# Routed expert weights: two loads for each of two matrices instead of one

## The chip, the cores and the metric

The kernel runs on one core of one Trainium2 chip. The metric is the device time of one execution in microseconds (us); lower is better. The profile that is shown is one execution, recorded by the hardware profiler. The engines are named as in the profile: PE is TensorE (matrix products), PEld its loads of the stationary operand, DVE VectorE, ACT ScalarE, POOL GpSimd, SP the engine that issues most DMA transfers. A "q" behind a name (SPq) means that engine's instruction queue: its issues and waits. DMA queue q1 is the one that SP's transfers go through, q0 the one of GpSimd's indirect transfers; both are carried by the same 16 DMA engines (the rings, below).

## What is computed

Two layers on 2048 tokens of 512 values, everything in 32-bit floats. The first layer is an RWKV recurrence gated by a two-expert feed-forward; the second is an attention gated by a mixture of experts. The change touches the loads of the mixture alone:

```python
h = relu(einsum('td,ndf->ntf', flat, shared_w1) + shared_b1[:, None, :])
shared_out = einsum('ntf,nfd->td', h, shared_w2) + shared_b2.sum(0)
out = flat + shared_out
scores = sigmoid(flat @ centroids.T) + bias
vals, idx = top_k(scores, KR)                      # KR = 4 of NR = 16 experts
gating = zeros_like(scores).at[arange(T)[:, None], idx].set(vals)
gating = gating / clip(gating.sum(-1, keepdims=True), 1e-08)
def step(acc, ew):
    w1, b1, w2, b2, g = ew                         # w1: 512 x 352, w2: 352 x 512
    hj = relu(flat @ w1 + b1)
    yj = hj @ w2 + b2
    return (acc + yj * g[:, None], None)
rout, _ = scan(step, zeros_like(flat), (routed_w1, routed_b1, routed_w2, routed_b2, gating.T))
return (out + rout).reshape(b, s, d)
```

The result of the layer is x + attention * silu(mixture).

## The kernel before

The kernel is written with a framework that takes tiles and their uses, puts the instructions of each engine in order by a planner with estimated costs, and adds the waits. Blocks under a runtime condition are kept as one piece.

The first layer takes the span up to about 900 us, the carrying over and the routing up to 1200, the shared experts and the keys of the attention up to 1350. Then comes the stage that matters here.

*Routed experts, 1353 to 1920 us.* Each token has four experts, so there are 2048 * 4 rows, sorted by expert into tiles of 128 rows in the DRAM tensor `xs`. There are at least 64 tiles (`FULL_TILES`) and at most 80 (`NRT`); the last ones run only if they are needed (L1722 and after). In this execution 73 results were written. For tile j, `hidden_rows(j)` (L1648):

- reads the number of the tile's expert into a register of SP;
- loads that expert's weights with `load1` (L650): `w1` as 128 partitions of 4 x 352 values (5632 B of each partition lie together in memory), `w2` as 128 partitions of 2 x 512 values (4096 B together), `w3`, the last 96 rows of the second matrix (2048 B each), and one row with the bias, in four transfers on SP's queue (L655 to L658). The pool `m1w` (L1527) holds three tiles' weights, so the load for tile j waits until tile j - 3 has been used: w1 until its product at L1676 is done, w2 and w3 until that at L1700 is done;
- loads the rows `x` (L1662, four buffers), turns them on PE (L1669), copies them (`xg`, L1671, ACT), multiplies by w1 in three parts of 128, 128 and 96 columns (L1676) with a relu on ACT behind each (`ht`, L935);
- makes on DVE each row's gate `g` (L1684) and its row number in the output (`to`, L1694, six buffers).

`down_rows(j)` (L1697), one tile later, multiplies by w2 and w3 (L1700), scales by the gate on DVE (`y`, L1705, four buffers), and adds the 128 rows to the DRAM tensor `comb` with an indirect DMA on GpSimd's queue (L1706), a read-modify-write in memory. Two tiles may add to the same row, so the framework lets these scatters follow each other one at a time.

Between the tiles stand 34 steps of the attention (`AHEAD`, L1712), which PE, ACT and DVE do in between; they have loads of their own on SP's queue (cosines and sines, L1333 and L1334, and `xo`, L1740).

`load1` is also called for the two shared experts in `behind_recurrence` (L665), at about 901 us, long before their use.

In memory, the weights are laid out by partition: `a["w1"]` is (18, 128, 4, 352), `a["w2"]` (18, 128, 3, 512).

Of the kernel before, what the change touches and what calls it, by code (L numbers as in the profile page):

```python
# [21 lines left out]
NC = D // P  # L22
# [45 lines left out]
NF1 = len(FCH)  # L68
# [9 lines left out]
def tile_kernel(ctx: ExitStack, tc: tile.TileContext, a: dict):  # L78
    nc = tc.nc
# [93 lines left out]
    for i in range(0, NT, 2):  # L173
        xin = n0.tile([P, 2, D], F32, tag="xin", bufs=NT // 2, name="xin")
        nc.sync.dma_start(
            out=xin, in_=a["x"][i * P : (i + 2) * P, :].rearrange("(n p) d -> p n d", p=P)
# [10 lines left out]
        out=wdc, in0=gate0_w[:, :, 1], in1=gate0_w[:, :, 0], op=ALU.subtract  # L187
    )
    wdp = n0ps.tile([P, NC, P], F32, tag="tp", name="wdp")
    for c in range(NC):  # L190
        dg = n0.tile([P, P], F32, tag="dg", bufs=2, name="dg")
        nc.vector.tensor_scalar(
            out=dg, in0=ident, scalar1=wdc[:, c : c + 1], scalar2=None, op0=ALU.mult
# [16 lines left out]
        out=upper, in_=upper, compare_op=ALU.is_gt, fill=0.0, base=0,  # L210
# [7 lines left out]
        out=eno, in0=col[:, 0:NST], scalar1=float(P), scalar2=None, op0=ALU.mult  # L218
# [3 lines left out]
    for i in range(0, NT, 2):  # L222
# [4 lines left out]
            out=shift, in0=mv[:, :, 0], scalar=-1.0, in1=rstd, op0=ALU.mult, op1=ALU.mult  # L227
# [3 lines left out]
        for j in range(2):  # L231
# [6 lines left out]
                out=junk, in0=xn, in1=wdiff, scale=1.0, scalar=0.0, op0=ALU.mult, op1=ALU.add,  # L238
                accum_out=dl[:, i + j : i + j + 1],
            )  # L240
    for i in range(NT):
# [10 lines left out]
        out=sel[:, :, 0], in0=dl, scalar1=0.0, scalar2=None, op0=ALU.is_le  # L252
    )
    nc.vector.tensor_scalar(
        out=sel[:, :, 1], in0=dl, scalar1=0.0, scalar2=None, op0=ALU.is_gt
# [3 lines left out]
        out=m, in0=dl, scalar=-1.0, in1=dl, op0=ALU.mult, op1=ALU.min  # L259
# [8 lines left out]
    for o, tri in ((0, upper), (N2, sums)):  # L268
        nc.tensor.matmul(
            out=tab[:, o : o + N2], lhsT=tri, rhs=sel.rearrange("p n e -> p (n e)"),  # L270
# [7 lines left out]
        out=run.rearrange("p e n -> p (e n)"), data0=newrow.rearrange("p e n -> p (e n)"),  # L278
# [8 lines left out]
        out=full, in0=own.to_broadcast([P, NT // 2]), in1=eno2[:, :, 1], op=ALU.is_gt  # L287
# [4 lines left out]
        out=paired[:, 0:1], in0=paired[:, 1:2], scalar1=2.0 * P, scalar2=None, op0=ALU.mult  # L292
    )
    nc.vector.tensor_tensor(
        out=pair_e[:, 0 : NSP - 1], in0=eno2[0:1, :, 0],
# [3 lines left out]
        out=pair_e[:, NSP - 1 : NSP], in0=own[0:1, :], in1=paired[0:1, 0:1], op=ALU.is_le  # L299
    )  # L300
    nc.vector.tensor_scalar(
        out=paired[:, 1:2], in0=paired[:, 0:1], scalar1=-1.0, scalar2=float(T),
# [4 lines left out]
        out=run[:, 1, :], in0=run[:, 1, :], scalar1=paired[:, 0:1], scalar2=None, op0=ALU.add  # L307
# [3 lines left out]
        out=row, in0=within, in1=run.rearrange("p e n -> p n e"), op=ALU.add  # L311
# [3 lines left out]
        out=alone, in0=row[:, :, 0], scalar1=paired[:, 0:1], scalar2=paired[:, 1:2],  # L315
# [10 lines left out]
        out=past, in0=bc(rowf, 2, C3), in1=bc(eno, 1, C3), op=ALU.is_ge  # L326
# [6 lines left out]
        out=place, in0=at, scalar=float(-P), in1=rowf, op0=ALU.mult, op1=ALU.add  # L333
    )
    nc.vector.tensor_tensor(
        out=past, in0=bc(at, 2, C3), in1=bc(col[:, 0:NST], 1, C3), op=ALU.is_equal
# [3 lines left out]
    for f in range(3):  # L340
        nc.vector.tensor_tensor(
            out=put[:, :, f, :], in0=past, in1=bc(facts[:, f, :], 2, C3), op=ALU.mult
# [3 lines left out]
    for i0 in range(0, NT, HN):  # L346
        hot = n0.tile([P, HN, P], F32, tag="hot", bufs=2, name="hot")
        nc.vector.tensor_tensor(
            out=hot, in0=bc(place[:, i0 : i0 + HN], 2, [P, HN, P]),
            in1=bc(col, 1, [P, HN, P]), op=ALU.is_equal,  # L350
        )
        for i in range(HN):
            nc.tensor.matmul(
                out=listed, lhsT=hot[:, i, :], rhs=put[:, i0 + i],
# [295 lines left out]
    def load1(pool, e, pick, row):  # L650

        w1 = pool.tile([P, NC, F1], F32, tag=f"w1{e}", name="w1")
        w2 = pool.tile([P, NF1 - 1, D], F32, tag=f"w2{e}", name="w2")
        w3 = pool.tile([P, D], F32, tag=f"w3{e}", name="w3")
        nc.sync.dma_start(out=w1, in_=pick(a["w1"]))  # L655
        nc.sync.dma_start(out=w2, in_=pick(a["w2"])[:, 0 : NF1 - 1, :])
        nc.sync.dma_start(out=w3[0:last, :], in_=pick(a["w2"])[0:last, NF1 - 1, :])
        nc.sync.dma_start(out=w3[last : last + 1, :], in_=row(a["b2"]))  # L658
        return w1, w2, w3
# [100 lines left out]
    for t_, fill in ((m_pool, 0.0), (n_pool, MASKED)):  # L760
        nc.gpsimd.affine_select(
            out=t_, in_=t_, compare_op=ALU.is_ge, fill=fill, base=1 - MB,
# [17 lines left out]
    for t_, fill in ((m_full, 0.0), *((t_, MASKED) for t_ in n_full)):  # L780
        own = t_[:, t_.shape[1] - P :]
        nc.gpsimd.affine_select(
            out=own, in_=own, compare_op=ALU.is_ge, fill=fill, base=0,
# [39 lines left out]
    for i in range(NT):  # L823
        yg = tr.tile([P, D], F32, tag="yg", bufs=6, name="yg")
        nc.gpsimd.indirect_dma_start(
            out=yg, out_offset=None, in_=ys0,
# [14 lines left out]
    for b in range(NRB):  # L841
# [4 lines left out]
        for s in range(n):  # L846
            nc.gpsimd.tensor_tensor(  # L847
                out=xr[:, s, :], in0=xr[:, s, :], in1=acc[:, i0 + s, 0:D], op=ALU.add
# [3 lines left out]
        for s in range(n):  # L852
            i = i0 + s
            nc.vector.tensor_scalar(
                out=acc[:, i, 0:D], in0=xr[:, s, :], scalar1=mv[:, s, 0:1],
# [3 lines left out]
        if (i + 1) % (TB // P) == 0:  # L859
            t0 = i + 1 - TB // P  # L860
            pl = m1y.tile([NR, TB], F32, tag="py", name="pl")
            for c in range(NC):
                nc.tensor.matmul(  # L863
                    out=pl, lhsT=cent[:, c, :], rhs=xT[:, c, t0 * P : (i + 1) * P],
# [10 lines left out]
    for b in range(NRB):  # L875
        rows2 = slice(b * RB, (b + 1) * RB)
        if b < PER:
            k0 = b * RB // MB
            nc.vector.tensor_reduce(
                out=xsum[:, :, k0 : k0 + RB // MB],  # L880
                in_=xT[:, :, rows2].rearrange("p c (n m) -> p c n m", m=MB),
                axis=AX.X, op=ALU.add,
            )
        else:
            nc.vector.tensor_reduce(
                out=xsum[:, :, NBLK : NBLK + 1],
                in_=xT[:, :, rows2].rearrange("p c (n m) -> p c n m", m=LW),
# [23 lines left out]
        out=upper, in_=upper, compare_op=ALU.is_gt, fill=0.0, base=0,  # L911
# [52 lines left out]
    with tc.tile_pool(name="rt", bufs=1, side="right") as rt, tc.tile_pool(  # L964
# [10 lines left out]
        for dst, tri in ((within, upper), (count, sums)):  # L975
            nc.tensor.matmul(
                out=dst.rearrange("p n e -> p (n e)"), lhsT=tri,
# [6 lines left out]
            out=run.rearrange("p e n -> p (e n)"), data0=newrow.rearrange("p e n -> p (e n)"),  # L984
# [5 lines left out]
            out=full, in0=run[:, :, NT - 1 : NT].to_broadcast([P, NR, NT]),  # L990
# [6 lines left out]
            out=end, data0=sums[:, 0:NR], data1=ntl, initial=0.0, op0=ALU.mult, op1=ALU.add  # L997
# [7 lines left out]
            out=run, in0=bc(first_tile, 2, [P, NR, NT]), scalar=float(P), in1=run,  # L1005
# [4 lines left out]
            out=row, in0=within, in1=run.rearrange("p e n -> p n e"), op=ALU.add  # L1010
# [3 lines left out]
        for k in range(KR):  # L1014
            one = rt2.tile([P, NT, NR], F32, tag="one", bufs=1, name="one")
            nc.vector.scalar_tensor_tensor(
                out=one, in0=rank, scalar=float(k + 1), in1=row, op0=ALU.is_equal, op1=ALU.mult,
# [10 lines left out]
            out=acc[:, :, D : D + NR], in0=row, in1=bc(tot, 2, [P, NT, NR]), op=ALU.mult  # L1028
# [5 lines left out]
        for i in range(NT):  # L1034
            for k in range(KR):
                ins = nc.gpsimd.indirect_dma_start(  # L1036
                    out=xs,
                    out_offset=bass.IndirectOffsetOnAxis(ap=slot[:, i, k : k + 1], axis=0),
                    in_=acc[:, i, :], in_offset=None,
# [21 lines left out]
        for m0 in (0, HM):  # L1061
# [4 lines left out]
                out=past, in0=bc(tno[:, ms], 2, sh3), in1=bc(end, 1, sh3), op=ALU.is_ge  # L1066
# [3 lines left out]
                out=te[:, ms], in0=te[:, ms], scalar1=float(NR - 1), scalar2=None, op0=ALU.min  # L1070
            )
            nc.vector.tensor_tensor(
                out=past, in0=bc(te[:, ms], 2, sh3), in1=bc(tno[:, 0:NR], 1, sh3),
# [6 lines left out]
            out=ohT, in0=te[0:NR, :], scalar1=part[0:NR, :], scalar2=None, op0=ALU.is_equal  # L1080
# [3 lines left out]
        for f in range(NF1):  # L1084
            nc.tensor.matmul(
                out=bt[:, f, :], lhsT=b1T[:, f * P : (f + 1) * P], rhs=ohT, start=True, stop=True,
# [26 lines left out]
    for w_, nm in ((wva, "Wv1"), (wks, "Wk_sem"), (wkg, "Wk_geo")):  # L1113
# [9 lines left out]
        out=ls, in0=ls, scalar1=DH ** -0.5, scalar2=None, op0=ALU.mult  # L1123
    )
    nc.vector.tensor_tensor(
        out=sm_sem, in0=ls.rearrange("p (g h) -> p g h", h=4),
# [3 lines left out]
        out=sm_geo, in0=ls.rearrange("p (g h) -> p g h", h=8),  # L1130
# [6 lines left out]
    for s_, n_ in ((slice(0, NBLK), MB), (slice(NBLK, NBLK + 1), LW)):  # L1137
        nc.vector.tensor_scalar(
            out=xk[:, :, s_], in0=xsum[:, :, s_], scalar1=1.0 / n_, scalar2=None, op0=ALU.mult,
# [8 lines left out]
    for c in range(NC):  # L1148
        ins = nc.tensor.matmul(
            out=pv, lhsT=xp[:, c].rearrange("p j k -> p (j k)"), rhs=wva[:, c, :],  # L1150
# [13 lines left out]
    for j in range(LW // P):  # L1164
        pl = kps.tile([P, HKV * DV], F32, tag="ps", name="pl")
        t0 = REMOTE + j * P
        for c in range(NC):
            nc.tensor.matmul(
                out=pl, lhsT=xT[:, c, t0 : t0 + P], rhs=wva[:, c, :],
# [22 lines left out]
    for u in range(2):  # L1192
# [9 lines left out]
        out=turn[:, :, DH : DH + HD], in0=id2[:, :, DH + HD :], scalar1=-1.0, scalar2=None,  # L1202
# [31 lines left out]
    for tb in range(NRB):  # L1234
        cols = slice(tb * RB, (tb + 1) * RB)
        pg = kps.tile([P, RB], F32, tag="ps", name="pg")
        for c in range(NC):
            nc.tensor.matmul(
                out=pg, lhsT=wkg[:, c, :], rhs=xT[:, c, cols],
# [4 lines left out]
        for j, nm in enumerate(("cos", "sin")):  # L1244
# [3 lines left out]
            if nrem:  # L1248
                nc.vector.tensor_reduce(
                    out=kg[:, j, b0 : b0 + nrem // MB],  # L1250
                    in_=tab[:, 0:nrem].rearrange("p (n m) -> p n m", m=MB), axis=AX.X, op=ALU.add,
# [9 lines left out]
        out=kgn, in0=kg[:, 1, 0:KP], scalar1=-1.0, scalar2=None, op0=ALU.mult  # L1261
# [604 lines left out]
```

## Time and profile before

| | |
|---|---|
| Median of 3 runs | 1981.4 us (1971.8 to 1984.0) |
| The profiled execution | 1987.5 us, span 1985.8 us |
| Granted TensorE clock, mean | 0.979 of full speed |
| PE, DVE, ACT, POOL busy | 94%, 39%, 27%, 19% of the span |
| DMA, whole span | 199488 packets, 381.35 MB, mean 192 GB/s |
| of these, q1 (SP) | 179800 packets, 332.78 MB, 50.8% of 16 engines' span |
| and q0 (GpSimd's indirect ones) | 18272 packets, 45.62 MB, 9.9% |
| Routed experts' stage, 1353 to 1920 us | 567 us |

How to read it: the page cuts the span into 40 slices of 49.6 us and gives a digit for each, the busy share in tenths. A packet in the DMA's counts is one contiguous run. The share of 16 engines is the time that all packets of a queue took, over 16 times the window's length; in a short window it can pass 100%, since a packet is counted where it starts or ends. The chain is followed back from the last instruction, at each step to what released it. Matmuls overlap each other, and their ends are modelled, so a PE that is shown busy is not at its peak for that.

### The profile page before, as it was taken

The page shows a single profiled execution, that of the slowest core. Times are in us where ns is not written, and L with a number is a line of the kernel's source. Part 1 is how long each engine was busy: PE and PEld are TensorE (multiplying, and loading weights), DVE is VectorE, ACT ScalarE, POOL GpSimd, SP SyncE. Part 2 cuts the span into 40 slices and gives each one's busy share as a digit, 9 for nine tenths or more (in the row PEclk, how much of TensorE's full clock was granted, in tenths as well). Part 3 has the DMA queues.
Part 4 walks back from the last instruction along what each step waited for, and adds up shares of the span by engine and source line. Part 5 has one row for each costly group of instructions (what it writes and reads, how often), then busy time and mean ns, then how long its engine had stood idle before and what let it go on. Part 6 is the DMA issues. An engine that isn't in the chain of part 4 may idle for free.

```text
span 1985.8 us, 23193 instructions
## 1 busy us (share of the span) xinstructions
PE 1869.7 (94%) x8107; PEld 1294.9 (65%) x8107; DVE 779.6 (39%) x1580; ACT 531.4 (27%) x1001; POOL 371.4 (19%) x293
## 2 busy tenths in 40 slices
PE   5899999999999999999889999999999999999857
PEld 4677777777877787777334644446776666676634
DVE  8444545362627263440256444502322222222117
ACT  5113132322324232321423122221222222222214
POOL 1211121120302120200621560001111121221120
PEclk9799999999999999999899999999999999999989
DMA  7647786536562535346532551028999999998944
GB/s 249 230 148 243 240 268 219 190 106 191 168 214 89 167 95 163 113 138 228 191 111 89 213 187 58 32 75 269 278 306 273 292 286 264 259 276 234 278 90 160
DMA packets 199488, 381.35 MB, mean 192 GB/s; under 512 B 15804, under 2 KB 106428, under 8 KB 198472
## 3 DMA queue, kind: packets, MB, share of 16 engines
q1 hardware_dynamic: 179800, 332.78, 50.8%
q0 software_dynamic: 18272, 45.62, 9.9%
q10 hardware_dynamic: 1296, 1.41, 0.2%
q8 instruction: 67, 1.10, 0.2%
q14 instruction: 53, 0.43, 0.1%
HBM read 294.04 MB, written 85.72 MB: 191 GB/s over the span
## 4 chain that ended last, share of the span: by engine, by line
PE 66%; DMA 21%; DVE 5%; issue 4%; POOL 2%; ACT 2%; SPq 0%; POOLq 0%; DVEq 0%; ACTq 0%
PE pg L567 23%; DMA comb<-y,to 17%; PE py L589 11%; PE proj L414 7%; PE py L1098 4%; PE ph L1676 4%; PE ph L949 3%; PE py L1700 3%; PE pw L1583 1%; PE pl L863 1%; PE pq L1342 1%; PE pw L1467 1%; PE pq L1398 1%; POOL xr L847 1%; PE po L1458 1%
## 5 line engine op out<-in xcount | busy, mean ns | idle before, releaser
L567 PE MATMUL pg<-xg,w 128*128 128x256 f32 (+1 forms) x2304 | 494.9, 367 | 0.0
L567 PEld LDWEIGHTS pg<-xg,w 128*128 128x128 f32 x2304 | 419.0, 190 | 90.1 <-issue 41.6
L1676 PEld LDWEIGHTS ph<-xg,w 128*128 128x128 f32 (+1 forms) x1776 | 224.3, 185 | 128.6 <-ACT ht L935 64.2
L1676 PE MATMUL ph<-xg,w 128*128 128x128 f32 (+1 forms) x1776 | 245.5, 282 | 29.3 <-ACT xg L1671 14.4
L589 PE MATMUL py<-wd,hT 128*128 128x512 f32 x544 | 256.9, 593 | 3.0 <-DVE hT L574 3.0
L1700 PE MATMUL py<-w,ht 128*128 128x512 f32 (+1 forms) x438 | 219.7, 602 | 0.0
L1706 POOL DMA_INDIRECT comb<-y,to x73 | 113.8, 1559 | 459.9 <-DVE to L1694 279.9
L574 DVE TENSOR_TENSOR hT<-sg,pg 128x256 f32<-128x256 f32 (+1 forms) x144 | 57.0, 401 | 329.9 <-ACT sg L572 329.8
L572 ACT ACTIVATE sg<-pg 128x256 f32<-128x256 f32 (+1 forms) x144 | 53.4, 371 | 412.2 <-PE pg L567 411.9
L935 ACT ACTIVATE ht<-ph,b1t 128x128 f32<-128x128 f32 (+1 forms) x222 | 81.1, 365 | 296.0 <-PE ph L1676 286.7
L589 PEld LDWEIGHTS py<-wd,hT 128*128 128x128 f32 x544 | 102.1, 190 | 72.2 <-issue 61.9
L1705 DVE TENSOR_SCALAR y<-py,g 128x512 f32<-128x512 f32 x73 | 54.5, 747 | 157.2 <-PE py L1700 104.6
L1694 DVE TENSOR_TENSOR to<-junk,away 128x1 int32<-128x1 f32 x74 | 11.8, 159 | 221.7 <-DMA comb<-y,to 220.9
L1098 PE MATMUL py<-w,hT 128*128 128x512 f32 (+1 forms) x192 | 89.3, 596 | 0.0
L1700 PEld LDWEIGHTS py<-w,ht 128*128 128x128 f32 (+1 forms) x438 | 72.2, 194 | 25.8 <-issue 24.4
L949 PE MATMUL ph<-xT,w 128*128 128x512 f32 (+1 forms) x192 | 88.0, 597 | 0.1
L1036 POOL DMA_INDIRECT xs<-acc,slot x64 | 63.4, 991 | 69.2 <-DMA xs<-acc,slot 45.5
L1671 ACT COPY xg<-tp 128x512 f32<-128x512 f32 x74 | 43.2, 584 | 101.6 <-PE tp L1669 99.2
L705 PE MATMUL po<-wo,yb 128*128 128x512 f32 x128 | 61.6, 637 | 8.4 <-DVE acc L838 4.4
L414 PE MATMUL proj<-xm,wk 128*128 128x256 f32 x256 | 59.4, 386 | 3.6 <-DVE xm L404 3.6
L1342 PE MATMUL pq<-xT,wqg 128*128 128x256 f32 x224 | 56.9, 390 | 5.5 <-PEq L1724 5.5
L414 PE MATMUL proj<-xm,wv 128*128 128x256 f32 x256 | 61.5, 394 | 0.0
(416 smaller groups left out, 2180.7 us busy)
## 6 DMA issues: line engine op xcount, KB each, us to landing
w<-in_w_dram SPq DMA_DIRECT2D x76, 704.0 KB
w<-in_w_dram SPq DMA_DIRECT2D x76, 512.0 KB
w<-in_w_gate_dram SPq DMA_DIRECT2D x72, 512.0 KB
w<-in_w_up_dram SPq DMA_DIRECT2D x72, 512.0 KB
wd<-in_w_down_dram SPq DMA_DIRECT2D x72, 512.0 KB
xs<-zero SPq DMA_DIRECT2D x16, 1360.0 KB
x<-xs SPq DMA_DIRECT2D x74, 272.0 KB
w<-in_w_dram SPq DMA_DIRECT2D x76, 192.0 KB
```

What stands on the lines that cost most here:

```text
L414: nc.tensor.matmul(out=ps[:, j, :], lhsT=w_[:, c, (o0 + j) * P : (o0 + j + 1) * P], rhs=xm[:, c, :], start=(c == 0), stop=(c == NC - 1),)
L567: nc.tensor.matmul(out=pg[:, i, 0:n], lhsT=w[:, c, i * FH + f * P : i * FH + (f + 1) * P], rhs=xg[:, c, 0:n], start=(c == 0), stop=(c == N ...
L589: nc.tensor.matmul(out=p, lhsT=hT[:, u * P : (u + 1) * P], rhs=wd[:, f, :], start=first_, stop=last_,)
L705: nc.tensor.matmul(out=po, lhsT=yb[:, c, s * P : (s + 1) * P], rhs=wo[:, c, :], start=(c == 0), stop=(c == NC - 1),)
L935: nc.scalar.activation(dst, src, AF.Relu, bias=b)
L949: nc.tensor.matmul(out=ph[0:n, :], lhsT=up(w, f, n, c), rhs=xT[:, c, cols], start=(c == 0), stop=(c == NC - 1),)
L1036: ins = nc.gpsimd.indirect_dma_start(out=xs, out_offset=bass.IndirectOffsetOnAxis(ap=slot[:, i, k : k + 1], axis=0), in_=acc[:, i, :], in_ ...
L1098: nc.tensor.matmul(out=py, lhsT=hT[0:n, e, f, s * P : (s + 1) * P], rhs=down(w, f, n), start=(e == 0 and f == 0), stop=(e == NS - 1 and f ...
L1342: nc.tensor.matmul(out=pq[:, j, :], lhsT=w[:, c, w0 : w0 + P], rhs=xT[:, c, tc0], start=(c == 0), stop=(c == NC - 1),)
L1676: nc.tensor.matmul(out=ph[0:n, f, :], lhsT=up(w, f, n, c), rhs=xg[:, c, :], start=(c == 0), stop=(c == NC - 1),)
L1700: nc.tensor.matmul(out=py, lhsT=hT[0:n, f, :], rhs=down(w, f, n), start=(f == 0), stop=(f == NF1 - 1),)
L1706: nc.gpsimd.indirect_dma_start(out=comb, out_offset=bass.IndirectOffsetOnAxis(ap=to, axis=0), in_=y, in_offset=None, compute_op=ALU.add,)
```

## The change

Inside `load1`, the one transfer for w1 becomes two, over the first two and the last two of its four blocks of 352 values, and the one for w2 becomes two, one for each block of 512 values. The longest run that lies together in memory and on the partition goes from 5632 to 2816 B for w1 and from 4096 to 2048 B for w2. Tiles, buffers, bytes and the products are the same; w3 and the bias row are loaded as before. The two shared experts' loads change in the same way.

```diff
         w1 = pool.tile([P, NC, F1], F32, tag=f"w1{e}", name="w1")
         w2 = pool.tile([P, NF1 - 1, D], F32, tag=f"w2{e}", name="w2")
         w3 = pool.tile([P, D], F32, tag=f"w3{e}", name="w3")
-        nc.sync.dma_start(out=w1, in_=pick(a["w1"]))
-        nc.sync.dma_start(out=w2, in_=pick(a["w2"])[:, 0 : NF1 - 1, :])
+        for c in range(0, NC, 2):
+            nc.sync.dma_start(out=w1[:, c : c + 2, :], in_=pick(a["w1"])[:, c : c + 2, :])
+        for f in range(NF1 - 1):
+            nc.sync.dma_start(out=w2[:, f, :], in_=pick(a["w2"])[:, f, :])
         nc.sync.dma_start(out=w3[0:last, :], in_=pick(a["w2"])[0:last, NF1 - 1, :])
         nc.sync.dma_start(out=w3[last : last + 1, :], in_=row(a["b2"]))
         return w1, w2, w3
```

## The prediction

> **What bounds the kernel now.** I read the slices of the span first, then the chain that ended last, the groups, the chain in order of time, and at last the DMA queues in short windows.
>
> ```profile
> PE   5899999999999999999889999999999999999857
> DMA  7647786536562535346532551028999999998944
> PE 66%; DMA 21%; DVE 5%; issue 4%; POOL 2%; ACT 2%; SPq 0%; POOLq 0%; DVEq 0%; ACTq 0%
> L1706 POOL DMA_INDIRECT comb<-y,to x73 | 113.8, 1559 | 459.9 <-DVE to L1694 279.9
> ```
>
> TensorE is busy nearly everywhere, but the DMA engines are at 90% or more in one stretch only, slices 28 to 37. That is the routed experts: 74 weight loads, from 1353 to 1920 us. All but 2 of the 76 calls that the change touches lie there. The last row is the scatter-add of a tile's result into comb; 17% of the whole chain lies on its transfers. The same chain in order of time (start, us, what), within the stretch and at its end, when no weights are loaded any more:
>
> ```profile
> 1596.48 7.04 DMA comb<-y,to
> 1604.25 6.11 DMA comb<-y,to
> 1611.09 7.63 DMA comb<-y,to
> 1619.45 6.44 DMA comb<-y,to
> 1626.62 8.25 DMA comb<-y,to
> ...
> 1896.68 4.66 DMA comb<-y,to
> 1902.10 4.85 DMA comb<-y,to
> 1907.71 5.01 DMA comb<-y,to
> ```
>
> The next scatter starts 0.73 us after the one before has landed: they go one at a time. In 1456 to 1920, 48 of the links are on the chain, 7.14 us each on average; alone they take 4.8. The load on the rings costs 2.3 us a scatter. The two tiles between the transposes at 1513.72 and 1527.15 took TensorE 6.7 us each without a gap, and 62 tiles in these 464 us take 7.5 each: scatters fall behind, four y buffers fill, VectorE waits (220.9 us for comb before `to`, by the wait table), then TensorE.
>
> Windows show what a scatter waits for. For the scatter issued at 1551.26, the rings carried weights alone (first row, 1554.76 to 1555.26), and its first runs come 4.0 us after the issue (next two rows, 1555.26 to 1555.76). The last row is 1898.48 to 1898.98: alone, the first run comes 1.8 us after the issue.
>
> ```profile
> q1 hardware_dynamic: 109, 0.19, 104.8%
> q1 hardware_dynamic: 92, 0.17, 97.9%
> q0 software_dynamic: 3, 0.01, 6.6%
> q0 software_dynamic: 16, 0.03, 80.8%
> ```
>
> In six more loaded scatters, looked at by half microseconds, the first run came 3.4 to 5.2 us after the issue. So most of the 2.3 us is the wait until the queue of GpSimd (q0) gets its first turn beside SP's (q1).
>
> **The change part by part.** It removes nothing and moves no step. Per expert tile, w1 (704 KB, 128 runs of 5632 B) becomes two transfers of 128 runs of 2816 B, and w2 (512 KB, 128 of 4096 B) two of 128 runs of 2048 B. Bytes stay the same.
>
> 1. *Issue on SP.* Transfers issued back to back stand 0.55 us apart (L655 at 1353.79, L656 at 1354.34, L657 at 1354.89). Two more: 1.1 us per tile. SP's shortest round is now 4.3 us (2.2 for four transfers, 1.0 to x, 1.1 back to w1) and becomes 5.4, under the 6.7 of TensorE. The cover is SP's own waiting, 153.9 + 50.8 us on L656 and L657 for the freed buffer. Behind it stand w3, the bias row, x, xo and cosine loads. Weights are asked for over two tiles ahead (13 us), land in 5 to 7, and TensorE waited 2.0 us for them in the whole stage. Priced at nothing; without cover 1.1 us x 73 = 80 us.
>
> 2. *Waits on TensorE.* A second counter to look at for w1 and for w2. The existing ones at L1676 and L1700 take 51 ns each: 0.10 us per tile where TensorE sets the pace (some 25 tiles: 2.5 us), hidden elsewhere. Ends: 0 and 73 x 0.10 = 7.5 us; I take 2.5.
>
> 3. *More runs on the rings.* 256 per tile, 16 per engine. The stage's start alone (1353 to 1366, weights only) and the first layer (600 to 700, mostly 1 KB runs):
>
> ```profile
> q1 hardware_dynamic: 1351, 4.40, 101.1%
> q1 hardware_dynamic: 9937, 13.53, 43.1%
> ```
>
> The first is 155.6 ns for 3257 B, the second 69.4 ns for 1362 B; a line through both is 7.5 ns per run plus 45 ns per KB. So 16 x 7.5 = 0.12 us per tile. Ends: zero, and the whole rate of the second row (19.6 against 20.9 B per ns, 6% more on some 3.6 us of w1 and w2, 0.22 us). I take 0.12, 9 us over 73 tiles if the rings were always the bound.
>
> 4. *Two more transfers' fixed part.* The same start: ten loads are issued from 1353.79 to 1359.10 and the rings move 4.40 MB in 13 us with no hole. The Trainium skill speaks against the change here: "DMA: Bandwidth & Descriptors", section "Anatomy of one DMA", gives each DMA some 2.0 us fixed and the rest by bytes at 436 GB/s, and "Rules for kernel authors" asks for transfers of 1 MiB. By it the loads of that window, standing one after the other, would need 10 x 2.0 + 10.1 = 30 us, and two more per tile would cost 2 x 2.0 x 73 = 292 us. The row says that fixed parts lie beside other transfers' bytes; I take the row, so nothing (ends 0 and 0.08 us per tile, what 101% leaves unseen).
>
> 5. *What a scatter waits for.* No row has these run lengths, so I bound it. Below: what a scatter waits for is bytes already fetched, gain 0. Above: the wait goes with the length of runs or transfers and halves. The nearest row is the row gather of the first layer, q0 again, beside 1 KB runs: issued at 249.17, first run 3.2 us later; the others 2.6 to 3.3. Against some 2.0 alone that is 1.0 of extra; beside 4 to 5.6 KB it is 2.7 (some 4.5 less 1.8). Straight between, at 2.4 KB: 1.6, so 1.1 us less for a fully loaded scatter, some 0.8 on average, as a few meet idle rings. 48 links x 0.8 = 38 us.
>
> 6. *What is late next.* Not all of that arrives: the rings fill up. In 1508 to 1548 they are full: q1 80.2%, q0 20.3%, for 6 tiles of weights and 4.65 scatters, 5.35 + 1.75 = 7.1 us of ring time per tile with its scatter. Over 1456 to 1920 q1 and q0 hold 67.3 + 22.0% of 464 us, 6.7 us for each of 62 tiles. The first counts the rings' own waiting at full load, the second hardly. With 0.12 added they are 7.2 and 6.8; since a scatter at 6.3 + 0.73 = 7.0 us lies between, I take 7.1 against the 7.5 that a tile takes now: 62 x 0.4 = 25 us. Less 0.12 x 11 = 1.3 for the tiles before 1456 (rings at 98%) and 2.5 from step 2: net 21 us.
>
> The profiled execution took 1987.5 us (span 1985.8), 6.1 above the median of 1981.4. 1987.5 - 21 = 1966.5; put on the median, 1960.
>
> **The rivals.**
> *B: the scatters gain nothing.* The wait is for bytes in flight. For it: gathers beside 1 KB runs still wait 1 us, a fifth of the length but more than a third of the wait. Against: 3.4 to 5.2 against 2.6 to 3.3 us to the first run. Left are steps 2 and 3 where they pace: 3 to 10 us, so 1981 to 1991.
>
> *C: slower, weights come late.* If the two queues take turns run by run, each turn of SP's queue now carries half; over a scatter's 8 rows per engine the weights lose 8 x 135 ns = 1.1 us, and SP asks 1.1 us later (step 1). The place is L1676, TensorE before its first product. It decides once the slack (13 - 7 = 6 us by the above) is under 2.2 us, as where SP hangs on a late py release. Half a microsecond on 50 tiles is 25 us: 2006, or 1996 if it is half as often. For it: rings at 98 to 101% leave nothing to catch up with. Against: 2.0 us of such waits now.
>
> *D: the framework's planner orders differently.* It orders by estimated costs; two more transfers may shift where attention steps and SP's x loads stand. Nothing in the profile tells the sign: 20 us either way.
>
> *E: a change in name only*, the two halves joined again on the rings: within 3 us of now. The 1 KB rows of the first layer are separate runs within one transfer, so I give it next to nothing and count it in B.
>
> **How the numbers follow.** A (steps 5 and 6) has 0.58, B 0.15, C 0.19, D 0.08. A's own range is 1940 (all 38 us of step 5, and a little of the waits behind them) to 1974 (the 7.2 us of step 6, with the upper ends of steps 2 and 3). About 1% (20 us) is what a measurement here can tell from no change: faster ends at 1961.6, slower starts at 2001. A gives 0.37 faster and 0.21 same, since its centre is just inside the border and its far side is the thinner one; B 0.15 same; C 0.06 same and 0.13 slower; D 0.03, 0.02, 0.03. Sum: 0.40, 0.44, 0.16. The time is A's, 1960. The range goes from 1938, the low end of A, up to 2002, which takes in B and the milder half of C; under 0.2 is left out.
>
> **What would show it.** A: scatters in 1456 to 1920 near 6.3 us, the first run of q0 3 to 4 us after the issue, fewer waits on comb, and a DMA share nearer to 1. B: 7.1 us as now. C: TensorE waits for w of 10 us and more at L1676. Step 3: ring time per byte of q1 up by 2%. Step 1: SP's waits at L656 shorter by about 1 us each. I am wrong above all if the first turn of q0 doesn't depend on the length of what is ahead, or if tiles stay at 7.5 us although scatters shrink.

## The result, and the profile after

The changed kernel takes 1966.3 us (median of 13 runs, 1957.3 to 1971.1); the kernel before, beside it, 1976.5 us (13 runs, 1971.8 to 1984.0). The ratio is 0.9942, 95% interval 0.9926 to 0.9959: some 10 us faster, 0.6%. The two profiled executions differ by more, 1987.5 to 1964.2 us: that of before lies 11 us above its median, that of after 2 us below its own. What is read below from this pair has the right places, but about twice the size.

Lines behind `load1` have numbers 2 higher after the change: the first product is L1678, the second L1702, the scatter L1708.

The page after: slices of TensorE and of the DMA engines, the chain's shares, and the scatter's group.

```profile
PE   4899999999999999999988999999999999999977
DMA  7647785635473434337441642025999999998953
PE 66%; DMA 21%; DVE 4%; issue 4%; ACT 2%; POOL 2%; SPq 0%; POOLq 0%; ACTq 0%; DVEq 0%
L1708 POOL DMA_INDIRECT comb<-y,to x73 | 114.3, 1566 | 434.7 <-DVE to L1696 220.8
```

The shares of the chain are about the same; the change shows in the length of the stage. The windows of the routed experts' stage, before and then after (window, its length, then busy time and instructions of PE, PEld, DVE, ACT and POOL, granted clock, DMA share, GB/s):

```profile
1353.00:1920.00 567.00, 531.86 (x2926) 380.53 (x2925) 138.69 (x484) 136.53 (x326) 111.68 (x72) 0.98 0.91 268
```

```profile
1353.00:1895.00 542.00, 521.91 (x2905) 373.11 (x2904) 135.98 (x480) 136.38 (x325) 112.46 (x72) 0.99 0.95 280
```

About the same work (the same 72 scatters) in 542 us instead of 567: all of the 23 us lies here, and the rings are fuller, 0.95 for 0.91. The chain of after in order of time, within the stage (start, us, what):

```profile
1502.82 5.59 DMA comb<-y,to
1509.14 6.97 DMA comb<-y,to
1516.85 6.67 DMA comb<-y,to
1524.25 6.53 DMA comb<-y,to
1531.52 6.47 DMA comb<-y,to
1538.72 8.15 DMA comb<-y,to
```

The scatters are still there, one after the other, but shorter: 6.53 us on average over the 51 links between 1456 and 1890, for 7.00 over 47 links before. (The prediction's 7.14 counts as one link the last piece of the stage, 13.68 us, in which the view merges two scatters.) 0.47 us off each of 51 links is 24 us, about what the pair of profiles differs by. The waits of VectorE for comb, before and after, and those of SP for a released buffer (in all us, times, longest):

```profile
DVE to L1694 <- DMA comb<-y,to: 220.9, 46, 8.3
DVE y L1705 <- DMA comb<-y,to: 48.0, 8, 7.5
```

```profile
DVE to L1696 <- DMA comb<-y,to: 198.3, 42, 7.7
```

```profile
SPq L656 <- PE py L1700: 153.9, 58, 8.6
SPq L657 <- PE py L1700: 50.8, 56, 7.7
```

```profile
SPq L658 <- PE py L1702: 96.1, 45, 6.2
SPq L659 <- PE py L1702: 13.3, 22, 1.7
```

VectorE waits 198.3 us for scatters instead of 268.9, SP 109 us for buffers of w2 and w3 instead of 205.

### The profile page after: what moved, and what is told of

Its sections match the earlier page's. It is cut to its first block, busy times and chain, and to the rows that moved or that the text cites. A ratio compares the mean times of both kernels' runs of the same rounds, so it can differ in the third digit from the quotient of the medians.

```text
span 1962.5 us, 23661 instructions
## 1 busy us (share of the span) xinstructions
PE 1865.3 (95%) x8107; PEld 1291.1 (66%) x8107; DVE 775.4 (40%) x1580; ACT 532.0 (27%) x1001; POOL 372.7 (19%) x293
## 3 DMA queue, kind: packets, MB, share of 16 engines
q1 hardware_dynamic: 201688, 332.79, 51.0%
## 4 chain that ended last, share of the span: by engine, by line
PE 66%; DMA 21%; DVE 4%; issue 4%; ACT 2%; POOL 2%; SPq 0%; POOLq 0%; ACTq 0%; DVEq 0%
PE pg L567 23%; DMA comb<-y,to 18%; PE py L589 11%; PE proj L414 8%; PE py L1100 4%; PE ph L951 3%; PE ph L1678 3%; PE py L1702 3%; PE pw L1585 1%; PE pl L865 1%; PE pw L1469 1%; DMA yg<-ys,slot 1%; PE pq L1400 1%; DVE st L126 1%; PE ps L1552 1%
## 5 line engine op out<-in xcount | busy, mean ns | idle before, releaser
L1678 PEld LDWEIGHTS ph<-xg,w 128*128 128x128 f32 (+1 forms) x1776 | 223.2, 183 | 119.2 <-ACT ht L937 56.5
L1678 PE MATMUL ph<-xg,w 128*128 128x128 f32 (+1 forms) x1776 | 244.7, 281 | 19.8 <-ACT xg L1673 9.8
L1702 PE MATMUL py<-w,ht 128*128 128x512 f32 (+1 forms) x438 | 218.2, 598 | 0.0
L1708 POOL DMA_INDIRECT comb<-y,to x73 | 114.3, 1566 | 434.7 <-DVE to L1696 220.8
L1696 DVE TENSOR_TENSOR to<-junk,away 128x1 int32<-128x1 f32 x74 | 11.7, 159 | 199.5 <-DMA comb<-y,to 198.3
L1702 PEld LDWEIGHTS py<-w,ht 128*128 128x128 f32 (+1 forms) x438 | 71.8, 193 | 25.3 <-issue 23.2
```

Of the source, the lines that this page charges most:

```text
L1678: nc.tensor.matmul(out=ph[0:n, f, :], lhsT=up(w, f, n, c), rhs=xg[:, c, :], start=(c == 0), stop=(c == NC - 1),)
L1702: nc.tensor.matmul(out=py, lhsT=hT[0:n, f, :], rhs=down(w, f, n), start=(f == 0), stop=(f == NF1 - 1),)
L1708: nc.gpsimd.indirect_dma_start(out=comb, out_offset=bass.IndirectOffsetOnAxis(ap=to, axis=0), in_=y, in_offset=None, compute_op=ALU.add,)
```

## The experiments

Five readings of the gain were put against each other. *T*: a scatter waits for the share that one queued transfer of weights has on a ring, so halved transfers halve the wait. *R*: it waits for runs of memory, so shorter runs do it. *O* (rival D of the prediction): the planner puts instructions in another order. *P1*: SP, with more to issue, asks for weights later. *P2*: transfers take turns at a few completion counters (SP's issues use eight semaphores in turn, in every kernel here), so smaller ones leave fewer bytes in flight. The expectations call P1 and P2 together P.

What was measured, in one table. "First run" is the time from a scatter's issue to the first half microsecond in which q0 moves three or more runs, a mean over the 54 to 67 scatters issued from 1402 to 1880 us; each such mean is good to some 0.25 us (0.1 in quarters, 0.02 in noload). "MB ahead" is what SP has issued and q1 has not begun to move 1.6 us after the scatter's issue, a mean over the same scatters; by then GpSimd's instruction, 1.55 us long, is over, and no run of a scatter has moved yet (the earliest, in any kernel, comes 2.12 us after the issue). Its zero is set where q1 stands still behind the last loads. "Per MB" is by how much the wait grows with each megabyte ahead (a straight line through the scatters of one kernel, the interval by resampling them). These three are worked out from the records of the DMA packets. The last column is VectorE's waiting for comb, in one trace each; it differs by 20 us and more between kernels that are equally fast (before, pause, short_pause). The ratio is to before, run beside each kernel, with its 95% interval.

| kernel | transfers w1, w2 | longest run, B | ratio | first run, us | MB ahead | per MB, us | comb, us |
| --- | --- | --- | --- | --- | --- | --- | --- |
| before | 1, 1 | 5632, 4096 | 1 | 3.64 | 0.77 | 2.00 (1.78 to 2.31) | 268.9 |
| one_short | 1, 1 | 2816, 2048 | 0.9981 (0.9962 to 1.0000) | 3.50 | 0.71 | 2.20 (2.06 to 2.38) | 219.5 |
| one_short4 | 1, 1 | 1408, 1024 | 0.9987 (0.9966 to 1.0008) | 3.53 | 0.77 | 2.07 (1.89 to 2.29) | 199.7 |
| w2_only | 1, 2 | 5632, 2048 | 0.9996 (0.9979 to 1.0014) | 3.57 | 0.75 | 2.24 (1.86 to 2.60) | 272.1 |
| w1_only | 2, 1 | 2816, 4096 | 0.9961 (0.9947 to 0.9974) | 3.47 | 0.69 | 2.08 (1.81 to 2.33) | 201.1 |
| after | 2, 2 | 2816, 2048 | 0.9942 (0.9926 to 0.9959) | 3.24 | 0.65 | 2.19 (1.96 to 2.41) | 198.3 |
| after_dep | 2, 2 | 2816, 2048 | 0.9915 (0.9885 to 0.9945) | 3.33 | 0.65 | 2.40 (2.17 to 2.67) | 174.3 |
| quarters | 4, 4 | 1408, 1024 | 0.9957 (0.9930 to 0.9984) | 2.88 | 0.48 | 2.18 (1.36 to 2.80) | 0.0 |
| pause | 1, 1 | 5632, 4096 | 1.0002 (0.9978 to 1.0026) | 3.50 | 0.73 | 1.99 (1.77 to 2.26) | 242.1 |
| short_pause | 1, 1 | 2816, 2048 | 0.9992 (0.9968 to 1.0016) | 3.51 | 0.76 | 1.94 (1.57 to 2.24) | 290.4 |
| bias3 | 1, 1 | 5632, 4096 | 0.9901 (0.9866 to 0.9935) | 3.14 | 0.59 | 2.47 (2.05 to 2.87) | 214.7 |
| aft_bias3 | 2, 2 | 2816, 2048 | 0.9871 (0.9836 to 0.9905) | 3.02 | 0.56 | 2.33 (1.95 to 2.75) | 0.0 |
| part_halves | 2, 2 | 5632, 4096 | 1.0407 (1.0377 to 1.0437) | 4.63 | 0.79 | 4.01 (3.74 to 4.28) | 0.0 |
| noload |  |  | 0.9817 (0.9779 to 0.9854) | 2.14 | 0.04 |  | 0.0 |

The wait per megabyte is the same, within its intervals, in the kernels with one, two and four transfers. One line through the scatters of all but part_halves is 1.95 us plus 2.09 us for each megabyte ahead (correlation 0.90), and it gives 3.57, 3.31 and 2.95 us for before, after and quarters. What falls, with the transfers cut, is the amount ahead: 0.77, 0.65, 0.48 MB. The first two of these overlap in their intervals (0.66 to 0.89 and 0.57 to 0.73); that of quarters (0.44 to 0.51) is clear of both. So a scatter's wait goes with the bytes ahead of it, and T, by which the wait for the same bytes would shrink with the size of a transfer, is not what the traces show.

### Shorter runs without more transfers: one_short, one_short4

The tiles get gaps of 32 B, so that one transfer has runs of the changed kernel's length (one_short), or of half of that (one_short4):

```diff
-        w1 = pool.tile([P, NC, F1], F32, tag=f"w1{e}", name="w1")
-        nc.sync.dma_start(out=w1, in_=pick(a["w1"]))
+        w1 = pool.tile([P, 2, NC // 2 * F1 + 8], F32, tag=f"w1{e}", name="w1")
+        nc.sync.dma_start(
+            out=w1[:, :, 0 : NC // 2 * F1],
+            in_=pick(a["w1"]).rearrange("p (r c) f -> p r (c f)", r=2),
+        )
...
```

> One transfer each for w1 and w2 as before, but the tiles in the on-chip memory have a gap of 32 B between halves, so the runs are 2816 and 2048 B. Instructions stand in the order of before on every engine. Theory R (a scatter waits for runs, so short runs alone bring the gain): ratio to before 0.994, scatters in the stage's main part 6.5 us as after, first run of the scatter's queue 3 to 4 us after the issue. Theory T (it waits for a whole transfer's share, so the number of transfers matters): ratio 1.000 to 1.004, scatters 7.2 us. Theory O (the planner's other order on TensorE brings the gain): ratio 1.000, scatters 7.2.

> As the run with one transfer each and a gap, but four runs each: 1408 and 1024 B. R: shorter still, ratio 0.985 to 0.992, scatters near 6 us, less 0.1 to 0.2 us per tile of ring time for 512 more runs. T and O: 1.000 to 1.008, scatters 7.2.

0.9981 and 0.9987: about a third of the change's gain (by the interval of one_short two thirds at most), and no more when the runs are halved once more. The first run comes 0.14 and 0.11 us sooner, against 0.40 in the changed kernel. What shorter runs cost is seen best where the rings carry weights alone. The DMA queue in 1353 to 1366, one_short and then the changed kernel (packets, MB, share of 16 engines):

```profile
q1 hardware_dynamic: 1862, 4.13, 101.2%
```

```profile
q1 hardware_dynamic: 1948, 4.13, 100.2%
```

Before moved 4.40 MB there: 6% less now, whether in one transfer or in two. It is no fixed price for each run, since one_short4, with twice as many runs again, moved 4.23 MB. Over 1402 to 1880 it is less: one run of w1 took 268 ns on its ring before, two runs in its place 270 in the changed kernel and 274 in one_short; for w2 it is 191, 196 and 198. R falls as the main cause.

### One matrix at a time: w1_only, w2_only

```diff
-        nc.sync.dma_start(out=w1, in_=pick(a["w1"]))
+        for c in range(0, NC, 2):
+            nc.sync.dma_start(out=w1[:, c : c + 2, :], in_=pick(a["w1"])[:, c : c + 2, :])
```

(and the same for w2 alone in w2_only.)

> Only w1 in two transfers (2816 B runs); TensorE's order is that of after. R: a bit over half the gain, 0.9965. T: the same, 0.9965. O: the whole gain, 0.994.

> Only w2 in two transfers (2048 B runs); TensorE's order is that of before. R and T: a bit under half the gain, 0.9975. O: 1.000.

w1 alone brings 0.39%, w2 alone 0.04%, together 0.43%; the change has 0.58% (0.41 to 0.74). So most of it is w1's, whose share of each of the 16 rings, 704 / 16 = 44 KB, is the largest of a tile's. That w2 brings so little while w1 stays whole was not tested further; the megabytes ahead of a scatter, 0.69 in w1_only and 0.75 in w2_only, go the same way.

### The order of before: after_dep

Splitting lets the planner think w1's first half lands sooner; in the changed kernel 30 of PE's 8107 instructions stand elsewhere (first products drawn forward). Here the first product of a tile also waits for the second half, and PE, DVE, ACT and POOL have before's order (on SP two loads of `xo` come later, as they do in w2_only, which gains nothing):

```diff
-                nc.tensor.matmul(
+                ins = nc.tensor.matmul(
...
+                if c == 0 and f == 0:
+                    tc.add_manual_dep(
+                        ins.ins, w[3].ins.name, AFTER, reason="both halves before the first"
+                    )
```

> The changed kernel, with one wait more: the first product of a tile waits for both halves of w1. With it the planner gives every engine the order of before; transfers and runs are those of after. O (the planner's other order brings the gain): ratio to before 1.000. T (a scatter waits for a whole transfer's share on a ring) and pacing P (more transfers to issue and 8 completion counters in turn hold SP back, so less lies ahead of a scatter): 0.994, intervals between scatters 7.4 us.

0.9915, at least as fast as the changed kernel. The gain comes with the order of before, so O is not its cause.

### More asking on SP: pause, short_pause

SP reads the expert's number a second time between w1 and w2; short_pause has the shorter runs of one_short as well.

```diff
+            e2 = nc.values_load(
+                tile_e[0:1, j : j + 1], engines=[mybir.EngineType.SP], min_val=0, max_val=NR - 1,
...
-        nc.sync.dma_start(out=w2, in_=pick(a["w2"])[:, 0 : NF1 - 1, :])
+        nc.sync.dma_start(out=w2, in_=(pick2 or pick)(a["w2"])[:, 0 : NF1 - 1, :])
```

> Before, but SP reads the expert's number a second time between the load of w1 and that of w2, some 1 us per tile, the issue time of the change without its transfers and runs. Every other engine keeps the order of before. P (SP asks later, so less lies on the rings ahead of a scatter): ratio 0.993 to 0.996, intervals between scatters 7.4 to 7.6 us, SP's waits on released buffers shorter by 1 us per tile. T (the share that one transfer puts on a ring): 1.000.

> One transfer each with the gap (runs of 2816 and 2048 B), and the same second read on SP; order of before. If P and R add up: 0.992, as in the changed kernel with the order of before (0.9915), intervals 7.4 us. If T is the cause: 0.998, as with the gap alone.

1.0002 and 0.9992: nothing, alone or with shorter runs. But the second read takes 0.3 us in the trace, not the 1 us of two issues that it was to stand for, and SP's waits for released buffers, 204.7 us before, are shorter by 0.2 us a tile and not by 1 (pause):

```profile
SPq L656 <- PE py L1705: 137.3, 55, 8.8
SPq L657 <- PE py L1705: 51.8, 56, 8.2
```

So 0.3 us of later asking brings nothing, and neither does the 0.55 us of w2_only's one more issue. P1 at its full size was not tested, and stays open.

### Twice the change: quarters

```diff
+        for c in range(NC):
+            nc.sync.dma_start(out=w1[:, c, :], in_=pick(a["w1"])[:, c, :])
+        for f in range(NF1 - 1):
+            for o in (slice(0, D // 2), slice(D // 2, D)):
+                nc.sync.dma_start(out=w2[:, f, o], in_=pick(a["w2"])[:, f, o])
```

> w1 and w2 in four transfers each, runs of 1408 and 1024 B. T: shares halve again, scatters' intervals 7.1 us or less, ratio 0.985 to 0.990, if SP holds: it must issue 11 transfers per tile, some 7.6 us. P: SP becomes the bound and weights come late: waits of TensorE for w over 20 us, ratio 1.00 or more. O: small, with some shift of the order here too.

The scatter's wait falls again, to 2.88 us, and VectorE no longer waits for comb at all, though GpSimd still does, for the scatter before. Yet the time is 0.9957, no better than the changed kernel's. SP's instructions in this kernel, one tile's round (start, us, what):

```profile
1600.05 2.20 SPq L659 DMA_DIRECT2D w<-in_w_dram  x4
1602.50 0.33 SPq L660 DMA_DIRECT2D w<-in_w_dram  x1
1603.03 0.28 SPq L661 DMA_DIRECT2D w<-in_b_dram  x1
1603.41 0.37 SPq L1665 DMA_DIRECT2D x<-xs  x1
1604.54 2.04 SPq L656 DMA_DIRECT2D w<-in_w_dram  x4
1606.86 1.91 SPq L659 DMA_DIRECT2D w<-in_w_dram  x4
```

From one w2 to the next it is 6.8 us, with hardly a gap: SP is next to being the bound. What is late, by the waits between 1330 and 1900 us:

```profile
POOL comb L1709 <- DMA comb<-y,to: 250.6, 44, 7.3
DVE junk L1687 <- DMA x<-xs: 239.9, 57, 8.6
PEld ph L1679 <- DMA w<-in_w_dram: 14.3, 27, 1.5
PE ph L1679 <- DMA w<-in_w_dram: 9.5, 14, 1.9
```

The rows x, which stand behind ten weight transfers on SP's queue, now come late, and weights too: on the chain of this kernel from 1456 to 1880, the transfers of w, x and `xo` hold 25% (w 12.9, x 8.7, `xo` 3.1), and those of comb next to nothing. That is rival C, at four transfers and not at two. (124 of TensorE's instructions and 28 of VectorE's stand elsewhere than in before, so the sizes are not of one cause.)

### Long runs, halved by partitions: part_halves

```diff
+        for o in (slice(0, P // 2), slice(P // 2, P)):
+            nc.sync.dma_start(out=w1[o], in_=pick(a["w1"])[o])
+        for o in (slice(0, P // 2), slice(P // 2, P)):
+            nc.sync.dma_start(out=w2[o], in_=pick(a["w2"])[o, 0 : NF1 - 1, :])
```

> w1 and w2 in two transfers each, but by halves of the partitions: 64 runs each of 5632 and 4096 B, so as many transfers as after and the same share of each on the rings in bytes, with the long runs of before. The planner's order differs from both. T and P: 0.994. R alone (runs matter) would be 1.000, and with the run with one transfer and a gap at 0.998 the most that R can hold is a third of the gain.

1.0407, 4% slower, but this doesn't speak against more transfers: VectorE waits for no scatter there, and TensorE 0.7 us for weights. TensorE's instructions, in before and then in part_halves (start, us, what, in brackets the idle time before):

```profile
1514.16 1.02 PE L1700 MATMUL py<-w,ht 128*128 128x512 f32 x2
1515.05 1.16 PE L1676 MATMUL ph<-xg,w 128*128 128x128 f32 x8
1516.05 1.02 PE L1700 MATMUL py<-w,ht 128*128 128x512 f32 x2
1516.91 1.05 PE L1676 MATMUL ph<-xg,w 128*128 128x128 f32 x8
```

```profile
1537.75 1.16 PE L1678 MATMUL ph<-xg,w 128*128 128x128 f32 x8 [0.73 <-ACT xg L1673]
1539.42 1.16 PE L1678 MATMUL ph<-xg,w 128*128 128x128 f32 x8 [0.52 <-ACT ht L937]
1541.10 1.11 PE L1678 MATMUL ph<-xg,w 128*96 128x128 f32 x8 [0.52 <-ACT ht L937]
1542.05 2.74 PE L1702 MATMUL py<-w,ht 128*128 128x512 f32 x6
```

Before, the second products of one tile stand between the parts of the next one's first products and cover ACT's relu. Here the planner put the six second products in one block, and TensorE waits for ACT at each part: 8.2 us a tile (1545.96 less 1537.75, the next tile's first part), where before took 6.7. So rival D did occur, in another kernel, and at 4%. That the rings also carried less (2.96 MB in 1353 to 1366 at 103.0%, for 4.40 MB) is a second difference, and a megabyte ahead costs a scatter 4.0 us here, so the kernel can't be set beside the others.

### The bias row in pieces: bias3, and both edits: aft_bias3

To have more transfers without touching w1 and w2, the bias row of 2 KB is loaded in three pieces.

```diff
-        nc.sync.dma_start(out=w3[last : last + 1, :], in_=row(a["b2"]))
+        for o in (slice(0, 128), slice(128, 256), slice(256, D)):
+            nc.sync.dma_start(out=w3[last : last + 1, o], in_=row(a["b2"])[:, o])
```

> Before, but the bias row is loaded in three pieces: two more transfers per tile to issue and count, as in the change, with w1 and w2 whole. The planner's order differs from both. P: 0.994. T: 1.000 to 1.003 (apart from what the order does).

0.9901, no less than the change itself. But its order is another one (2060 of PE's 8107 instructions and 110 of DVE's 1580 stand elsewhere; SP's loads of x stand one after each tile's bias row, not in clumps), and its trace shows another path. The waits of bias3 between 1330 and 1920 us:

```profile
DVE y L1706 <- DMA comb<-y,to: 190.1, 35, 8.3
DVE to L1695 <- DMA comb<-y,to: 24.6, 5, 7.6
```

The wait for scatters has moved from `to` to `y`, and is 214.7 us in all. A megabyte ahead costs a scatter about as much as before, but less lies ahead, 0.59 MB for 0.77, with w1 and w2 whole; its first run comes at 3.14 us. That could be the spacing of SP's issues (three pieces of the bias row take 1.15 us to issue, one took 0.28), or fewer bytes in flight (P2). How much of bias3's gain is order and how much is either of these stays open.

> The changed kernel with the bias row of each expert loaded in three pieces as well, so that both edits that were faster than before stand in one kernel. If halved transfers of w1 and w2 shorten the scatter's wait for its first turn, and the three pieces gain by something else (the order that the planner gives them, with the loads of x spread out), the two add up: 0.984 of before or a little above, scatters on the chain at or under 6.3 us, and the wait for the first run rises with the megabytes ahead at some 0.6 us each as in the changed kernel. If both take the same time out of the same wait, or TensorE's 6.7 us per tile comes next, it stays at the better one of the two: 0.990 to 0.994. If two more issues on SP are now too many (eight transfers per tile), TensorE waits for weights and it is slower than the changed kernel: 0.996 or above.

0.9871, and 1948.7 us (6 runs, 1945.9 to 1960.4): the fastest kernel that computes the whole, 1.3% under before. VectorE doesn't wait for comb any more (GpSimd still does, 255.6 us). The window 1456 to 1850, before and then aft_bias3:

```profile
1456.00:1850.00 394.00, 373.81 (x2055) 268.25 (x2054) 99.49 (x344) 94.77 (x227) 78.31 (x51) 0.97 0.93 274
```

```profile
1456.00:1850.00 394.00, 387.62 (x2162) 274.42 (x2161) 98.93 (x360) 101.08 (x241) 83.72 (x54) 1.00 0.97 282
```

TensorE is busy for 387.6 of 394 us, from 373.8. The product of the two ratios would be 0.984, inside the interval. The wait per megabyte, expected at 0.6 us, is a miss. That figure had counted the megabytes ahead at the scatter's issue, 1.6 us too early: taken there, such slopes are flatter, scatter widely and differ between the kernels. At the end of the issue it is 2.33 us here and 2.19 in the changed kernel; what is lower is the amount ahead, 0.56 MB.

### No weight loads: noload

```diff
-            w = weights()
+            w = kept[j % FIRST]
```

> The kernel before with the routed experts' weights loaded for the first three tiles only and used again for all the others, so the weights of the right expert are left out from the fourth tile on. It shows what all weight loads together cost the scatters, and so how much of that the change took back. If what a scatter waits for is the weights' transfers ahead of it on the rings, its first run comes about 2 us after the issue, scatters on the chain take some 4.8 to 5.2 us, their interval falls under 6.7 us, and TensorE sets the pace: 62 tiles x (7.5 - 6.7) = 50 us less, 0.975 of before or somewhat lower, since TensorE's clock is the only thing left that could take some of it back. If the scatters are slow by themselves when they follow each other among busy engines, they stay at 6.5 us or above and the time is within 1% of before.

0.9817: all weight loads together cost some 36 us, of which the change took back 10 and aft_bias3 some 25. A scatter's first run comes 2.14 us after its issue. The same window:

```profile
1456.00:1850.00 394.00, 388.76 (x2183) 278.58 (x2182) 104.07 (x356) 102.90 (x244) 86.31 (x56) 1.00 0.43 79
```

TensorE is busy 98.7% of it with the rings at 0.43, and scatters follow each other every 7.10 us on average; before it was 7.79, after 7.33, in aft_bias3 7.30. So 7.1 us per tile, with the attention's steps among them, is TensorE's own floor in this stage.

The granted clock differs too: in this window it is 0.97 before, 0.99 after, 1.00 in aft_bias3 and noload. Among before's 109 runs beside the experiments, a run with 0.001 more of mean clock took 0.86 us less (0.46 to 1.26). By this, as an estimate, the clock goes with 2 us of the 16 that after_dep gains (its mean is 0.9814, before's 0.9792), but with some 6.5 us of the gains of aft_bias3 and noload (0.9873 and 0.9875, for 0.9798). Whether the clock is higher because TensorE stops less often was not tested.

## Why the prediction held, and what was off

**What bounds the kernel** was right: the scatters, one at a time and late for their turn beside the weights. noload shows it: without the loads their wait falls from 3.64 to 2.14 us, and TensorE sets the pace.

**Step 1** (issue on SP, priced at nothing) held. SP's waits for released buffers became 95 us shorter, 1.3 us for each of 73 tiles, and TensorE waited 2.9 us for weights in the whole stage. The cover is real, and quarters shows its end.

**Step 2** (2.5 us on TensorE) is under what the runs resolve: after_dep adds a dependence on the second half, and is no slower.

**Step 3** (7.5 ns for each additional run) was on the high side for the stage as a whole: over 1402 to 1880 the changed kernel's packets show 1.4 ns for each additional run of w1 and 4.4 for w2. Its upper end, 6%, came at the stage's start, where the rings carry weights alone: 4.13 MB against 4.40. q1's ring time over the span didn't rise by the 2% expected: 51.0% of 1962.5 us is 1001 us per engine, 50.8% of 1985.8 was 1009.

```profile
q1 hardware_dynamic: 201688, 332.79, 51.0%
```

**Step 4** (fixed parts of more transfers lie beside others' bytes) held. It had weighed 2.0 us for each additional transfer, from the Trainium skill; added up, that would have cost 292 us here and three times as much in quarters, and both are faster than before. The section that it names, of the page "DMA: Bandwidth & Descriptors", gives the figure for transfers that GpSimd issues, and these are SP's; no run here shows what one of SP's costs alone.

**Step 5** is the term that was mis-sized. It took 0.8 us off a scatter's wait, 38 us over 48 links, by a line between run lengths of 1 KB and of 4 to 5.6 KB. The first run came 0.40 us sooner on average (3.64 to 3.24, each good to some 0.25). The seven scatters that it had looked at, 3.4 to 5.2 us, were loaded ones, above the mean of all. And the length of runs was the wrong variable: one_short has it, without more transfers, and gets 0.14 us and 0.2%. What the wait goes with is the megabytes ahead, about 2.1 us for each in before and after alike, and the change lowers these. The step's upper bound had named "runs or transfers" together, so that the forecast came near in time owes something to luck. The row gather that it took as its nearest row lies in another stage with other transfers ahead, and differs in more than the runs.

**Step 6** expected 7.1 us per tile, 21 us net. In the profiled pair scatters follow each other every 7.79 and then 7.33 us (1456 to 1850), but by the medians 10 us remain. The 7.1 us was put down to the rings being full; noload has the same value at half-empty rings, so TensorE's own floor lies there too, and the 6.7 us read from two tiles was too low as its pace.

**The rivals.** B (scatters gain nothing) fell in its outcome, 7.00 to 6.53 us, but its premise, that the wait is for bytes in flight, is what the traces show; it had overlooked that the change leaves fewer of them. C (weights late) didn't occur with two transfers and did with four. D was excluded here by after_dep, and is real elsewhere. E (the halves joined again) fell: q1 moves 201688 packets for 179800. Of what would show A, the scatters' 6.3 us came out at 6.53; a first run at 3 to 4 us could not tell, since it is 3.64 before and 3.24 after.

**What stays open.** Cutting the transfers in two, at the order of before, is shown to bring the gain, and shorter runs to bring 0.2%, by their interval 0.4 at most. A scatter's wait is seen to go with the megabytes ahead of it, and these to be fewer with more transfers. Why they are fewer is not shown: that SP's transfers take turns at eight counters (P2) would do it, and the most that lies on the rings at once falls from 2.15 MB over 1.71 to 1.46 with two and four transfers; that SP asks for some of the weights later (P1) would do it too. Neither was tried by itself at full size, and bias3 shows that the same wait shortens with w1 and w2 whole.

## What to carry to other kernels

Where a small serial transfer on one queue stands beside a stream of large loads on another, look at the time from its issue to its first run and at how many bytes lie ahead of it then, and try the loads in more transfers, as long as the issuing engine has waiting to spare; stop where its round nears the tile's time. Before a gain or a loss is put down to the transfers, compare the order of instructions: here an edit of a load alone moved the planner to orders worth 4% to the bad. And measure the floor without the loads first, since it says how much there is to have.

## What the runs showed of the hardware

- The first turn of a queue beside a loaded one comes later by about 2.1 us for each megabyte that the loaded one still has ahead, over some 2 us with nothing ahead, and no difference is seen between transfers of 704 and 512 KB, halves and quarters of them (2.00, 2.19 and 2.18 us per MB, all to 128 partitions). At the stage's 280 GB/s a megabyte takes 3.6 us (an estimate), so a scatter does not wait until all of it has moved.
- The same loads cut into more transfers left less ahead: 0.77 MB with one each, 0.65 with two, 0.48 with four. The first turn came after 3.64, 3.24 and 2.88 us, and after 2.14 with no loads. Shorter runs in one transfer changed it by 0.1 us.
- Runs of 2816 and 2048 B for 5632 and 4096 moved 6% fewer bytes where the rings carried weights alone, and took 1 and 2% more ring time where two queues share them.
- Transfers to 64 partitions, with the same long runs, moved 2.96 MB in a window where those to 128 moved 4.40, both with the rings shown full (103.0% and 101.1%).
